# A four-layer convolution stack on one core: order of the first pair's statistics, and of work inside the last pair's layers 2 and 3

## The chip, the core and the metric

The kernel runs on one core of one Trainium2 chip. A core has four engines that compute side by side, each with its own instruction queue: PE (TensorE, matrix products; its loads of weights are listed apart as PEld), DVE (VectorE), ACT (ScalarE) and POOL (GpSimd). SP issues most of the DMAs. The metric is the time of one execution on the device in microseconds, the median of several runs. All data are float32.

## What is computed

The input is a batch of 8 images of 64 channels and 128 x 128 pixels. Four layers follow each other, each added to its input, and each fed with a group norm (32 groups, so two channels of one image share mean and variance):

```python
# layer 0: "adder" 3x3 convolution, for every output channel o
x = x + relu(b[o] - sum(abs(patch - w[o])))
# layer 1: per channel, silu and a cubic B-spline of 8 coefficients
x = x + scale_base * silu(v) + scale_sp * spline(v) + bias
# layer 2: Haar transform to four subbands, depthwise 3x3, pointwise 4C x 4C,
#          3x3 convolution 4C x 4C, gelu, inverse Haar
t = conv(conv(depthwise(haar(v)), pw_w), cv_w)
x = x + haar_inverse(gelu(t))
# layer 3: nearest of 512 codes of 64 channels for every pixel
d = (v*v).sum() + (e*e).sum() - 2 * (v @ e.T)
x = x + e[argmin(d)]
```

Each group norm needs the statistics of the whole image before the first element of its layer can be computed.

## The kernel before

Two images of 64 channels fill the 128 partitions, so the batch is four pairs, taken one after the other by `run` (L1233). An image of 128 rows is cut into NCH = 8 chunks of R = 16 rows for all but layer 0, which uses chunks of 32 rows.

**The frame.** `setup` (L120) prepares the weights of all layers inside one memory pool named setup (L187): first the constants and layer 0's weights and bias (w0, w0o, b0, up to L209), then layer 1's (cf, l1w, stored to DRAM at L261), layer 2's (cvn and pwn are loaded, 36 blocks are copied to wsrc, transposed on PE and copied back to cvt, L302 to L305; the pointwise and the 3x3 weights are multiplied to w2, L318, and w2 is stored to DRAM, L321; then gam, L335), and the code book (embT, esq_half, L345 to L359). After setup, `run` takes the statistics of pair 0: `raw_norm` (L397) loads the raw image in 8 tiles of 1 MB through three buffers (L403), takes bn_stats of each (L419) and combines them to mean and inverse deviation in mr (`group_norm_steps`, L433). It loads the first chunk of layer 0 into x0 and normalizes it there (`pad_first`, L508). Then each pair goes through layer 0 (`layer0`, L512) and layer 1 (`layer1`, L698). For all pairs but the last, layers 2 and 3 and the raw statistics of the next pair run as small steps in between the next pair's layer 0 (`layer2_beside`, `layer3_beside`), at steps written out by hand. The last pair has no layer 0 after it, so its layers 2 and 3 run alone, in `layer2` (L804) and `layer3` (L915).

**Who sets the order.** In layer 0 the instructions of PE, ACT and DVE stay in the order of the program. Elsewhere the framework plans the order for each engine when it builds the kernel: it walks through a time of its own estimate and, when an engine is free, takes the instruction that comes first in the program among those that it deems ready. A later instruction can so be put ahead of an earlier one that would still wait; the chip then carries out that order whatever really comes first. Memory of a pool that is closed is given to the pools opened after it.

**Layer 2 of the last pair.** For each chunk, `transform` (L836) makes the four subbands (8 rows of 64 columns each) in `sub`, a padded tile with a border row above and below, two of them in turn. `border` (L832, POOL copies) fills border rows from the neighbouring chunk. `depthwise` (L849) takes 9 operations for each subband, one scaling and eight multiply-adds, over 8 rows into `dw`. The first and last row of dw that the 3x3 convolution needs beyond the chunk are again copied by `border` from the neighbour's dw. `convolve` (L862) accumulates 9 taps x 4 subbands x 2 images for each half of the output channels (oab), each product of 64 x 512; taps are the outer loop, subbands the inner one:

```python
for n, (di, dj, w) in enumerate(taps):
    for k in range(4):
        for i, rows in enumerate(images):
            v = dw[rows, k, di : di + G, dj : dj + S]
            nc.tensor.matmul(ps[:, i], self.w2[rows, k, w, oab, :], v, ...)
```

In the trace each such product is two instructions. `inverse` (L882) is another 16 products and four additions into x. The loop (L893 on) makes the transform of chunk j + 1 and the depthwise of chunk j before the convolution of chunk j - 1.

**Layer 3 of the last pair.** For each chunk, x is normalized to xn (DVE), squared to sq (ACT), and 16 products with two columns sum the squares over channels (px, PE, L929), which DVE halves to xsq (L931). Then, for each of 16 rows and both images: a product with the code book into ps (PE, L938; four PSUM buffers, pool pd), t = half the code's square plus xsq (ACT, L941), nd = ps - t with its maximum (DVE, L944), the index of the maximum ix (DVE, L946), and a gather of the codes into g by POOL (L947). After each row the gathered codes of both images are transposed on PE into q (L955), and after each fourth row DVE adds q to x (L958). The chunk is stored at its end.

Of the kernel before, what the change touches and what calls it, by code (L numbers as in the profile page):

```python
# [22 lines left out]
C = 64  # L23
# [77 lines left out]
class Net:  # L101
    def __init__(self, ctx, tc, x, w0, b0, coef, sbase, ssp, bias1, dw_w, dw_b, pw_w, pw_b, cv_w, cv_b, embed, out):
        self.tc, self.nc = tc, tc.nc
        self.embed = embed
        self.n_pairs = x.shape[0] // 2
        self.x_dram = x.rearrange("(n two) c h w -> n (two c) (h w)", two=2)
        self.out_dram = out.rearrange("(n two) c h w -> n (two c) (h w)", two=2)
        self.dram = ctx.enter_context(tc.tile_pool(name="dram", bufs=1, space=bass.MemoryType.DRAM))
        self.const = ctx.enter_context(tc.tile_pool(name="const", bufs=1))
        self.small = ctx.enter_context(tc.tile_pool(name="small", bufs=2))  # L110
        self.s_of = [self.dram.tile([2, RA + 2, W + 2], F32, name=f"s{n}_dram") for n in range(2)]
        self.x_of = [self.dram.tile([P, H * W], F32, name=f"x{n}_dram") for n in range(3)]
        self.setup(w0, b0, coef, sbase, ssp, bias1, dw_w, dw_b, pw_w, pw_b, cv_w, cv_b, embed)
# [6 lines left out]
    def setup(self, w0, b0, coef, sbase, ssp, bias1, dw_w, dw_b, pw_w, pw_b, cv_w, cv_b, embed):  # L120
# [66 lines left out]
        with tc.tile_pool(name="setup", bufs=1) as sp, tc.tile_pool(name="setup_ps", bufs=2, space=PSUM) as pp:  # L187
# [13 lines left out]
            for n in range(len(PLANS)):  # L201
# [7 lines left out]
                nc.vector.tensor_tensor(self.b0[:, n], ws, braw, ALU.add)  # L209

# [593 lines left out]
    def layer2(self, mr, stats):  # L804


        nc, tc = self.nc, self.tc
# [5 lines left out]
        with ExitStack() as ctx:  # L813
# [9 lines left out]
            def padded(name, bufs, j):  # L823
                t = sp.tile([P, 4, G + 2, S + 2], F32, name=name, tag=name, bufs=bufs)
                nc.gpsimd.memset(t[:, :, :, 0 : S + 2 : S + 1], 0.0)
                if j == 0:
                    nc.gpsimd.memset(t[:, :, 0, 1 : S + 1], 0.0)
                if j == NCH - 1:
                    nc.gpsimd.memset(t[:, :, G + 1, 1 : S + 1], 0.0)
                return t  # L830

            def border(above, below):  # L832
                nc.gpsimd.tensor_copy(above[:, :, G + 1, 1 : S + 1], below[:, :, 1, 1 : S + 1])
                nc.gpsimd.tensor_copy(below[:, :, 0, 1 : S + 1], above[:, :, G, 1 : S + 1])

            def transform(j):  # L836
                t = padded("sub", 2, j)
                xv = self.x[j]
                s, d = (sp.tile([P, R, S], F32, name=n) for n in ("hs", "hd"))
                nc.vector.tensor_tensor(s, xv[:, :, 0:W:2], xv[:, :, 1:W:2], ALU.add)  # L840
                nc.vector.tensor_tensor(d, xv[:, :, 0:W:2], xv[:, :, 1:W:2], ALU.subtract)
                at = (slice(1, G + 1), slice(1, S + 1))
                nc.vector.scalar_tensor_tensor(t[:, 0, at[0], at[1]], s[:, 0:R:2], m4, s[:, 1:R:2], ALU.add, ALU.add)
                nc.vector.tensor_tensor(t[:, 1, at[0], at[1]], s[:, 0:R:2], s[:, 1:R:2], ALU.subtract)
                nc.vector.tensor_tensor(t[:, 2, at[0], at[1]], d[:, 0:R:2], d[:, 1:R:2], ALU.add)
                nc.vector.tensor_tensor(t[:, 3, at[0], at[1]], d[:, 0:R:2], d[:, 1:R:2], ALU.subtract)
                return t

            def depthwise(j, sub):  # L849
                t = padded("dw", 3, j)  # L850
                for k in range(4):
                    out = t[:, k, 1 : G + 1, 1 : S + 1]
                    for n, (di, dj, w) in enumerate(taps):
                        v = sub[:, k, di : di + G, dj : dj + S]
# [7 lines left out]
            def convolve(j, dw, oab):  # L862
# [6 lines left out]
                for n, (di, dj, w) in enumerate(taps):  # L869
                    for k in range(4):  # L870
# [3 lines left out]
                    if n == 0:  # L874
# [18 lines left out]
            sub = transform(0)  # L893
            dw = late = None
            for j in range(NCH + 1):
                done = dw
                if j < NCH:
                    if j + 1 < NCH:
                        below = transform(j + 1)
                        border(sub, below)  # L900
                    dw = depthwise(j, sub)
                    sub = below
                    if j > 0:
                        border(done, dw)
                if j > 0:
                    gs = [convolve(j - 1, done, 0)]
                    if late is not None:
                        inverse(*late)
                    gs.append(convolve(j - 1, done, 1))
                    late = (j - 1, gs)  # L910
# [4 lines left out]
    def layer3(self, mr, pair):  # L915
        nc, tc = self.nc, self.tc
        with ExitStack() as ctx:
# [4 lines left out]
            for j in range(NCH):  # L922
                xn = sp.tile([P, R, W], F32, name="xn")
                self.normalize(xn, self.x[j], mr)
                sq = sp.tile([P, R, W], F32, name="sq")
                nc.scalar.activation(sq, xn, AF.Square)
                px = pq.tile([P, 2 * R], F32, name="px", tag="px")
                for r in range(R):
                    nc.tensor.matmul(px[:, 2 * r : 2 * r + 2], sq[:, r, :], self.per_image, start=True, stop=True)  # L929
                xsq = sp.tile([P, 2 * R], F32, name="xsq")  # L930
                nc.vector.tensor_scalar(xsq, px, 0.5, None, ALU.mult)  # L931
                for r in range(R):
                    g = tp.tile([P, 2, C], F32, name="g")
                    for img in range(2):
                        rows = slice(img * C, (img + 1) * C)
                        n = 2 * r + img
                        ps = pd.tile([P, NE], F32, name="ps")
                        nc.tensor.matmul(ps, xn[rows, r, :], self.embT[rows, :], start=True, stop=True)  # L938
                        t = tp.tile([P, NE], F32, name="t")

                        nc.scalar.activation(t, self.esq_half, AF.Identity, bias=xsq[:, n : n + 1])  # L941
                        nd = tp.tile([P, NE], F32, name="nd")
                        mx = self.best[:, n % NB, :]
                        nc.vector.tensor_tensor_reduce(nd, ps, t, 1.0, -FAR, ALU.subtract, ALU.max, mx[:, 0:1])  # L944
                        ix = tp.tile([P, 8], U32, name="ix")
                        nc.vector.max_index(ix, mx, nd)  # L946
                        nc.gpsimd.indirect_dma_start(  # L947
                            out=g[:, img, :],
                            out_offset=None,
                            in_=self.embed,  # L950
                            in_offset=bass.IndirectOffsetOnAxis(ap=ix[:, 0:1], axis=0),
                        )
                    if r % 4 == 0:
                        q = pq.tile([P, 4, W], F32, name="q", tag="q")
                    nc.tensor.transpose(q[:, r % 4, :], g.rearrange("p i c -> p (i c)"), self.ident)  # L955
                    if r % 4 == 3:
                        v = self.x[j][:, r - 3 : r + 1, :]
                        nc.vector.tensor_tensor(v, v, q, ALU.add)  # L958
                cols = slice(j * R * W, (j + 1) * R * W)
                nc.sync.dma_start(out=self.out_dram[pair][:, cols], in_=self.x[j].rearrange("p r w -> p (r w)"))  # L960
# [272 lines left out]
    def run(self):  # L1233
        tc = self.tc
        mr = self.mr_tile()
        later = None
        with ExitStack() as first:
            self.x0 = first.enter_context(tc.tile_pool(name="x0", bufs=1)).tile([P, (RA + 2) * (W + 2)], F32, name="x0")
            for _ in self.raw_norm(0, mr):
                pass  # L1240
            self.load_chunk(0, 0, self.x0)
            self.pad_first(mr)
            for pair in range(self.n_pairs):
                last = pair + 1 == self.n_pairs
                stats, nxt = self.stats_tile(), self.mr_tile()
                raw, count = (iter(()), 2) if last else (self.raw_norm(pair + 1, nxt), 2 * NCH + 8)
                plans = [3] + [1] * 7 + [2] * 6 + [0] * 2 if later else [0] * NP
                counts = [TILES[n] // 2 if n else 0 for n in plans[:-2]] + [count // 2] * 2
                if later is None:
                    self.layer0(pair, mr, stats, BUFS_ALONE, lambda p: (plans[p], raw, counts[p]))  # L1250
                else:
                    with tc.tile_pool(name="between", bufs=1) as bp:
                        between = bp.tile([P, NCH * 4, 6], F32, name="between")
                        steps = chain(self.layer2_beside(later, between, sum(counts[:8])), self.layer3_beside(between, pair - 1, sum(counts[8:-2])), raw)
                        self.layer0(pair, mr, stats, BUFS_BESIDE, lambda p: (plans[p], steps, counts[p]))
                if last:
                    first.close()
                else:
# [45 lines left out]
```

## Time and profile before

| | us |
|---|---|
| median of 3 runs (19237.88 to 19248.91) | 19244.84 |
| the profiled execution | 19248.76 |
| its span, first to last instruction | 19247.0 |
| first operation of layer 0 (ACT) starts at | 133.48 |
| layer 2 of the last pair, about | 18168 to 18800 |
| layer 3 of the last pair, about | 18800 to 19247 |

Busy time in these stretches, and the mean clock granted to PE (1 is full speed):

| stretch, us | PE | DVE | ACT | POOL | clock |
|---|---|---|---|---|---|
| 0 to 133 | 58.4 | 55.4 | 22.5 | 13.4 | 0.86 |
| 133 to 4000 | 3825.0 | 3799.2 | 3677.2 | 196.2 | 1.00 |
| 18168 to 18800 | 586.3 | 273.6 | 19.1 | 28.3 | 0.97 |
| 18800 to 19247 | 392.9 | 362.7 | 185.3 | 245.8 | 0.59 |

The page gives busy time per engine, the chain of waits followed back from the last instruction, and groups of instructions with their mean duration and the idle time ahead of them. A record of an instruction is named by its line, engine and operation, with what it writes and reads. PE's matrix products are pipelined and their ends are modelled, so a PE that is busy all the time may still work slowly.

### The profile page before, as it was taken

To read this page: it belongs to the slowest core of one execution; us is meant where nothing else is said; L and a number is where in the kernel's file an instruction comes from. 1 tells how busy PE (TensorE), PEld (TensorE's weight loads), DVE (VectorE), ACT (ScalarE), POOL (GpSimd) and SP (SyncE) were. 2 spreads that over 40 slices of the span, in tenths; PEclk is the share of its full clock that TensorE was granted. 3 is DMA by queue.
4 is the path that set the end of the run, shared out by engine and by line. 5 is a ranking of instruction groups with operands and counts; after the bars stand their busy time and mean duration, and the time that the engine had idled before them with its cause. 6 is when DMAs were issued, how large, how long until landed. Compare 5 with 4: busy or idle time off the path is not lost.

```text
span 19247.0 us, 328577 instructions
## 1 busy us (share of the span) xinstructions
PE 18582.4 (97%) x145850; PEld 5795.2 (30%) x145850; DVE 17869.9 (93%) x13785; ACT 17302.3 (90%) x6401; POOL 2775.6 (14%) x1698
## 2 busy tenths in 40 slices
PE   8999999999999999999999999999999999999898
PEld 2333233233233222222223222222232322222343
DVE  8999999989999999998999999998899999999837
ACT  7999999889999999988999999998999999999603
POOL 0000000000000344200000034420000004441005
PEclk9999999999999999999999999999999999999996
DMA  1000000121111000021111100002011110000101
GB/s 52 6 11 10 6 12 8 43 63 37 36 33 37 20 20 27 26 73 35 34 41 35 33 15 24 24 28 82 28 33 38 35 33 19 23 22 16 59 1 35
DMA packets 412639, 584.02 MB, mean 30 GB/s; under 512 B 64080, under 2 KB 309456, under 8 KB 385744
## 3 DMA queue, kind: packets, MB, share of 16 engines
q1 hardware_dynamic: 355408, 497.90, 8.6%
q0 software_dynamic: 55808, 65.11, 1.9%
q8 instruction: 1142, 18.71, 0.4%
q14 instruction: 281, 2.30, 0.0%
HBM read 439.55 MB, written 123.25 MB: 29 GB/s over the span
## 4 chain that ended last, share of the span: by engine, by line
PE 54%; DVE 27%; issue 9%; ACT 8%; DMA 1%; POOL 0%; SPq 0%; DVEq 0%; ACTq 0%; POOLq 0%
PE ps L691 39%; DVE buf L624 12%; DVE buf L628 9%; ACT buf L622 7%; PE cv L1066 5%; PE pa L787 2%; PE pb L787 2%; PE ps L873 2%; DVE dw L1043 1%; DVE ix L1193 1%; DVE nd L1191 1%; PE ps L938 1%; DVE x L624 1%; PE py L1089 1%; PE pd L1179 1%
## 5 line engine op out<-in xcount | busy, mean ns | idle before, releaser
L691 PE MATMUL ps<-buf,sel 128*32 128x512 f32 x116336 | 13032.1, 598 | 358.4 <-DVE buf L628 233.4
L622 ACT ACTIVATE buf<-buf,w 128x4096 f32<-128x4096 f32 x1980 | 7212.9, 3708 | 305.9 <-PE ps L691 299.5
L622 ACT ACTIVATE buf<-x,w 128x4096 f32<-128x4096 f32 x1938 | 7044.5, 3708 | 376.5 <-PE ps L691 290.8
L691 PEld LDWEIGHTS ps<-buf,sel 128*32 128x32 f32 x116336 | 3642.9, 110 | 9338.4 <-issue 7867.1
L624 DVE TENSOR_SCALAR buf<-buf,w 128x4096 f32<-128x4096 f32 x1795 | 4162.7, 2357 | 193.7 <-PE ps L691 192.9
L624 DVE TENSOR_SCALAR buf<-x,w 128x4096 f32<-128x4096 f32 x1558 | 3640.1, 2367 | 284.3 <-PE ps L691 274.5
L628 DVE SCALAR_TENSOR_TENSOR buf<-buf,w,buf 128x2048 f32<-128x2048 f32 x1262 | 2913.5, 2349 | 23.0
L628 DVE SCALAR_TENSOR_TENSOR buf<-x,w,buf 128x2048 f32<-128x2048 f32 x1072 | 2475.3, 2349 | 19.7
L1194 POOL DMA_INDIRECT g<-in_L_conv_embed_weight,ix x768 | 1825.6, 2377 | 2849.3 <-issue 1432.4
L602 POOL DMA_DIRECT2D y<-in_x x480 | 608.3, 2072 | 9442.6 <-ACT y L589 6467.9
L1066 PE MATMUL cv<-dw,w2s 64*128 64x512 f32 x6912 | 1655.2, 607 | 3.3 <-issue 3.3
L622 ACT ACTIVATE x<-buf,w 128x4096 f32<-128x4096 f32 x396 | 1468.6, 3709 | 60.8 <-PE ps L691 60.7
L691 PE MATMUL ps<-x,sel 128*32 128x512 f32 x10832 | 1302.8, 595 | 27.1 <-DVE x L628 18.9
L1066 PEld LDWEIGHTS cv<-dw,w2s 64*128 64x128 f32 x6912 | 628.0, 186 | 1025.4 <-issue 1012.0
L624 DVE TENSOR_SCALAR x<-buf,w 128x4096 f32<-128x4096 f32 x281 | 660.2, 2349 | 24.4 <-PE ps L691 24.2
L691 PEld LDWEIGHTS ps<-x,sel 128*32 128x32 f32 x10832 | 352.6, 110 | 849.1 <-issue 742.7
L1043 DVE SCALAR_TENSOR_TENSOR dw<-sub,dws,dw 128x512 f32<-128x512 f32 (+2 forms) x768 | 574.9, 749 | 10.6
L873 PE MATMUL ps<-dw,w 64*128 64x512 f32 x2304 | 525.5, 597 | 29.4 <-DVE dw L859 20.4
L1191 DVE CUSTOM_DVE_ANT_0 nd<-pd,t 128x512 f32<-128x512 f32 x768 | 520.0, 677 | 30.5 <-ACT t L1181 30.4
L1193 DVE FIND_INDEX8 ix<-best,nd 128x8 uint32<-128x512 f32 x768 | 526.1, 685 | 0.1
L776 DVE TENSOR_TENSOR r<-r,r 128x1024 f32<-128x1024 f32 x384 | 455.0, 1219 | 76.1 <-ACT r L775 76.1
L1179 PE MATMUL pd<-embT,xn 64*128 64x512 f32 x1536 | 491.4, 650 | 30.0 <-DVE best L1191 29.6
(220 smaller groups left out, 7961.3 us busy)
## 6 DMA issues: line engine op xcount, KB each, us to landing
w2s<-w_dram SPq DMA_DIRECT2D x576, 192.0 KB
xd<-x_dram SPq DMA_DIRECT2D x256, 256.0 KB
x<-x_dram SPq DMA_DIRECT2D x56, 1024.0 KB
raw<-in_x SPq DMA_DIRECT2D x32, 1024.0 KB
x_dram<-y SPq DMA_DIRECT2D x512, 64.0 KB
out<-x SPq DMA_DIRECT2D x32, 1024.0 KB
y<-in_x POOLq DMA_DIRECT2D x480, 64.0 KB, 4.2
x_dram<-x SPq DMA_DIRECT2D x24, 1024.0 KB
```

The lines of the kernel that those rows point to most:

```text
L622: nc.scalar.activation(ab, tap(j, ts[0]), AF.Abs, bias=w[:, ts[0] : ts[0] + 1], scale=-1.0)
L624: nc.vector.tensor_scalar(ab, tap(j, ts[0]), w[:, ts[0] : ts[0] + 1], None, ALU.max)
L628: nc.vector.scalar_tensor_tensor(at, tap(j, t, h), w[:, t : t + 1], at, ALU.max, ALU.add)
L691: nc.tensor.matmul(at, sel[:, M - 1 - m : 3 * M - 1 - m], rhs, start=(n == first[p]), stop=(n + 1 == first[p + 1]))
L787: nc.tensor.matmul(to[images[i], q, :], dspl[:, k, ws[i], :], cubes[i][:, cols], start=(p == 0), stop=stop)
L873: nc.tensor.matmul(ps[:, i], self.w2[rows, k, w, oab, :], v, start=(n == 0 and k == 0), stop=(n == 8 and k == 3))
L1043: nc.vector.scalar_tensor_tensor(out, v, wt, out, ALU.mult, ALU.add)
L1066: nc.tensor.matmul(ps[:, i], weights[r, w // 3, :], v, start=(k == 0 and n == 0), stop=(k == 3 and n == 8))
L1179: nc.tensor.matmul(ps, xns[j][at, r, :], self.embT[at, :], start=True, stop=True)
L1191: nc.vector.tensor_tensor_reduce(nd, ps, t, 1.0, -FAR, ALU.subtract, ALU.max, mx[:, 0:1])
L1193: nc.vector.max_index(ix, mx, nd)
L1194: nc.gpsimd.indirect_dma_start(out=g[:, img, :], out_offset=None, in_=self.embed, in_offset=bass.IndirectOffsetOnAxis(ap=ix[:, 0:1], axis=0),)
```

## The change

It has three parts. (1) The statistics of the first pair, the load of x0 and its normalization move from `run` into `setup`, right after layer 0's bias and ahead of the weights of layers 1 to 3; x0's pool is opened before setup. (2) In layer 2 of the last pair `sub` becomes one tile that reaches four image rows (two subband rows) into the next chunk, and `depthwise` of chunk 0 covers one row more, of later chunks the same number shifted by one; a chunk's first two dw rows are copied from the chunk before. The depthwise of chunk j + 1 is issued before the convolution of chunk j, and subbands become the outer loop of the convolution. (3) In layer 3 of the last pair the sums of squares of chunk j + 1 are issued at row 6 of chunk j (`prepare`) and taken at row 12 (`take_squares`); the transposes and the addition of four rows come six rows after the last of them (`add`, LATE = 6), with 12 buffers of g instead of 4 and 8 of ix.

```diff
@@ __init__
+        self.first = ctx.enter_context(ExitStack())
+        self.x0 = self.first.enter_context(tc.tile_pool(name="x0", bufs=1)).tile([P, (RA + 2) * (W + 2)], F32, name="x0")
         self.setup(w0, b0, coef, sbase, ssp, bias1, dw_w, dw_b, pw_w, pw_b, cv_w, cv_b, embed)
@@ setup, after the bias b0
+            self.mr0 = self.mr_tile()
+            for _ in self.raw_norm(0, self.mr0):
+                pass
+            self.load_chunk(0, 0, self.x0)
+            self.pad_first(self.mr0)
@@ layer2
-            def padded(name, bufs, j):
...
-            def border(above, below):
-                nc.gpsimd.tensor_copy(above[:, :, G + 1, 1 : S + 1], below[:, :, 1, 1 : S + 1])
-                nc.gpsimd.tensor_copy(below[:, :, 0, 1 : S + 1], above[:, :, G, 1 : S + 1])
+            sub = sp.tile([P, 4, G + 3, S + 2], F32, name="sub")
+            dws_of = [sp.tile([P, 4, G + 2, S + 2], F32, name=f"dw{n}") for n in range(3)]
+            for t in [sub] + dws_of:
                 nc.gpsimd.memset(t[:, :, :, 0 : S + 2 : S + 1], 0.0)
+            for t in (sub, dws_of[0]):
+                nc.gpsimd.memset(t[:, :, 0, 1 : S + 1], 0.0)
+            inner = slice(1, S + 1)
+
+            def transform(j):
+                if j > 0:
+                    nc.vector.tensor_copy(sub[:, :, 1:3, inner], sub[:, :, G + 1 : G + 3, inner])
+                row = 3 if j else 1
+                for n, lo, hi in ((j, 4 if j else 0, R), (j + 1, 0, 4)):
+                    if n == NCH:
+                        nc.vector.memset(sub[:, :, row, inner], 0.0)
+                        continue
+                    xv = self.x[n][:, lo:hi]
+                    s, d = (sp.tile([P, R, S], F32, name=name)[:, 0 : hi - lo] for name in ("hs", "hd"))
+                    nc.vector.tensor_tensor(s, xv[:, :, 0:W:2], xv[:, :, 1:W:2], ALU.add)
+                    nc.vector.tensor_tensor(d, xv[:, :, 0:W:2], xv[:, :, 1:W:2], ALU.subtract)
...
+            def depthwise(j):
+                t = dws_of[j % 3]
+                if j > 0:
+                    nc.gpsimd.tensor_copy(t[:, :, 0:2, inner], dws_of[(j - 1) % 3][:, :, G : G + 2, inner])
                 if j == NCH - 1:
+                    nc.gpsimd.memset(t[:, :, G + 1, inner], 0.0)
+                at, n_rows = (1, G + 1) if j == 0 else (2, G - 1 if j == NCH - 1 else G)
                 for k in range(4):
-                    out = t[:, k, 1 : G + 1, 1 : S + 1]
+                    out = t[:, k, at : at + n_rows, inner]
                     for n, (di, dj, w) in enumerate(taps):
-                        v = sub[:, k, di : di + G, dj : dj + S]
+                        v = sub[:, k, at - 1 + di : at - 1 + di + n_rows, dj : dj + S]
...
-                for n, (di, dj, w) in enumerate(taps):
-                    for k in range(4):
+                for k in range(4):
+                    for n, (di, dj, w) in enumerate(taps):
...
-                    if n == 0:
+                    if k == 0:
                         for r, c, e in ends:
...
+            transform(0)
+            dw = depthwise(0)
+            late = None
+            for j in range(NCH):
                 done = dw
+                if j + 1 < NCH:
+                    transform(j + 1)
+                    dw = depthwise(j + 1)
+                gs = [convolve(j, done, 0)]
+                if late is not None:
+                    inverse(*late)
+                gs.append(convolve(j, done, 1))
+                late = (j, gs)
             inverse(*late)
@@ layer3: normalize, Square and the px products move into prepare(j), the
@@ halving into take_squares(j), the body of the row loop into nearest(j, r)
+                g = gs[j, r] = tp.tile([P, 2, C], F32, name="g", bufs=LATE + 6)
...
+                    ix = tp.tile([P, 8], U32, name="ix", bufs=8)
...
+            def add(j, r):
+                q = pq.tile([P, 4, W], F32, name="q", tag="q")
+                for n in range(4):
+                    nc.tensor.transpose(q[:, n, :], gs.pop((j, r + n)).rearrange("p i c -> p (i c)"), self.ident)
+                v = self.x[j][:, r : r + 4, :]
+                nc.vector.tensor_tensor(v, v, q, ALU.add)
+                if r + 4 == R:
+                    cols = slice(j * R * W, (j + 1) * R * W)
+                    nc.sync.dma_start(out=self.out_dram[pair][:, cols], in_=self.x[j].rearrange("p r w -> p (r w)"))
+
+            prepare(0)
+            take_squares(0)
+            for n in range(NCH * R + LATE):
+                j, r = divmod(n, R)
+                if j + 1 < NCH and r in (6, 12):
+                    (prepare if r == 6 else take_squares)(j + 1)
+                if j < NCH:
+                    nearest(j, r)
+                if n >= LATE + 3 and (n - LATE - 3) % 4 == 0:
+                    add(*divmod(n - LATE - 3, R))
@@ run: the loop over pairs is unchanged but for the lines moved to setup
-        mr = self.mr_tile()
-        later = None
-        with ExitStack() as first:
-            self.x0 = first.enter_context(tc.tile_pool(name="x0", bufs=1)).tile([P, (RA + 2) * (W + 2)], F32, name="x0")
-            for _ in self.raw_norm(0, mr):
-                pass
-            self.load_chunk(0, 0, self.x0)
-            self.pad_first(mr)
+        mr, later = self.mr0, None
```

## The prediction

> **What bounds the kernel now.** I read the page first, then the busy time by stage, then the three places that the diff touches.
>
> ```profile
> span 19247.0 us, 328577 instructions
> PE 18582.4 (97%) x145850; PEld 5795.2 (30%) x145850; DVE 17869.9 (93%) x13785; ACT 17302.3 (90%) x6401; POOL 2775.6 (14%) x1698
> PEclk9999999999999999999999999999999999999996
> ```
>
> The lines are busy time, share of the span and instructions of each engine, and the clock granted to PE in tenths, in 40 slices. Three engines are nearly full, but that is layer 0, which the diff leaves alone; only the last slice, with layer 3 in it, has a low clock. The windows by stage give what it can reach: 133 us before the first layer-0 operation, 632 us of layer 2 of the last pair (18168 to 18800), 447 us of its layer 3 (to 19247). These parts follow each other, so a microsecond saved in one is one saved in all.
>
> Start. The chain of waits over the first 140 us (start, us, what):
>
> ```profile
> 85.04 7.93 PE gp L335 x36
> ...
> 96.35 1.59 PE ep L357 x2
> 97.96 4.68 DMA raw<-in_x
> ...
> 116.95 13.80 DMA x<-in_x
> 130.85 2.56 DVE x L485
> 133.48 3.72 ACT buf L622
> ```
>
> The weights of all layers are prepared first, up to 97.9; only then do the raw image and its statistics come, and layer 0 starts at 133.48. The DMA queue's own waits say why the image is late (us in total, times, longest):
>
> ```profile
> SPq L321 <- ACT w L319: 40.3, 1, 40.3
> SPq L403 <- DMA w_dram<-w: 11.9, 1, 11.9
> ```
>
> The raw loads (L403) are queued behind the store of w2, and their buffers lie in memory that the setup pool gives back only at its end: the store has landed and ep is done at 97.9, and so are both waits.
>
> Layer 2. PE by itself, in order of time (start, us, and in brackets its idle time before and who ended it):
>
> ```profile
> 18194.35 5.38 PE L873 MATMUL ps<-dw,w 64*128 64x512 f32 x16 [14.52 <-DVE dw L859]
> 18205.61 3.79 PE L873 MATMUL ps<-dw,w 64*128 64x512 f32 x8 [5.88 <-DVE dw L859]
> ...
> 18237.02 14.81 PE L873 MATMUL ps<-dw,w 64*128 64x512 f32 x56 [8.95 <-POOL dw L833]
> ```
>
> The sums of chunk 0 start at 18194.35 and stop twice: with the tap as outer loop the first taps want all four subbands, and the taps of the last row want a border row which is copied from chunk 1. From 18252 to the last inverse PE hardly waits (541 busy of 544 us).
>
> Layer 3. Who waited for whom, 18800 to the end, and one repeated place of PE and DVE:
>
> ```profile
> DVE x L958 <- PE q L955: 34.7, 29, 4.3
> ...
> DVE nd L944 <- PE ps L938: 32.3, 7, 4.8
> ```
> ```profile
> 18871.81 6.98 PE L929 MATMUL px<-per_image,sq 128*128 128x2 f32 x32
> ...
> 18878.72 2.08 PE L938 MATMUL ps<-embT,xn 64*128 64x512 f32 x4
> ...
> 18880.94 0.69 DVE L944 CUSTOM_DVE_ANT_0 nd<-ps,t 128x512 f32<-128x512 f32 x1 [4.58 <-PE ps L938]
> ```
>
> DVE is the engine that does the work here: two nd and two ix per row come every 2.54 us. It loses 34.7 us to additions that are queued before their codes have arrived, and 32.3 us to PE, which needs 6.98 us for one chunk's sums of squares while DVE has only four ready products (pd, four buffers) to live on. The px blocks come every 54.2 us ((19142.78 - 18871.81) / 5).
>
> **The Trainium skill.** "DMA: Bandwidth & Descriptors", Bandwidth, Measured: 1 MB from HBM takes 6.15 us, 341 GB/s. Here 100 to 120 us moves 383 GB/s, a little more; I use that. "TensorE: Matmul & The Clock Gate", Part 1: the array runs at half clock until it has been busy for a window of some 3.4 us. Layer 2 agrees: a clock of 0.67 until 18205, 0.82 to 18252, 1.00 after. In layer 3 it is 0.59, although PE's row there is hardly ever empty, so I don't count on a release. "Perfetto Trace Analysis", Optimization Strategy: a gap that repeats can mean too few buffers. The 4.58 us gap, the same at each chunk, is such a one, and the change adds no pd buffer. "SBUF — State Buffer", Who interferes with whom: a DVE instruction with two SBUF inputs contends with a GpSimd read. POOL's copies of 128x256 do spread from 0.40 to 2.47 us beside L859.
>
> **The change, part by part.**
>
> Start: nothing is added; 8 raw loads, 32 bn_stats, the group norm, the load of x0 and its normalization move ahead of the other weights. The block that is exposed now is 133.48 - 97.96 = 35.5 us, and that is the most that can go. Least: nothing, if the weights are pushed back by as much. On SP the loads go past all later weight loads (cvn among them), and past the store of l1w, for which SP already stands 5.7 us. On POOL go x0's memsets (three seen, 0.16 to 0.21 us each) and the power of mr (0.58 us), between setup's own, which are done by 13.3 us; PE gets two small products (0.56 us) and the wait for the statistics in front of them, behind which tp and wp may stand. That risk is in the delay below. Once w0o is in (19.4), 8 raw (8.4 MB), x0 (2.2 MB) and the remaining weights (about 3 MB) at 0.383 MB/us take 36 us, to about 55; bn_stats of a tile takes 2.47 us, as long as its load, so DVE is nearly full until then, with wsrc (L302, 8.7 us), l1w and the like in the gaps. The first cvn was used at 38.8, and from there to ep it is 59 us, nearly all PE. I put that first use at about 51, so setup ends at 110, layer 0 starts at 111, and the part saves 22 us (0 to 35). The rest of x0's 13.8 us is hidden with it. Layer 0's other buffers still wait for the setup pool's end.
>
> Layer 2: chunk 0 now reaches one row further (128x576), so it needs no row of chunk 1. STT of that shape takes 0.818 us in the second pair's L1043 against 0.748, so it starts every 0.735 instead of 0.668. With k outermost PE can start when subbands 0 and 1 are done (the planner runs them in pairs, as now): 2 x 0.56 + 16 x 0.735 = 12.9 us after dw begins. dw begins at 18183.0 now, after parts of chunk 1's transform (hs and hd, some 2.4 us, and three sub, some 1.9) have run between the steps of the group norm; in their place come six small operations of 128 to 256 elements, some 2 us, so about 2 us earlier: PE starts at 18193.7. The 72 products of k = 0 and 1 take 15.5 us, by when k = 2 and 3 are ready. The 160 products until 18252.0 took 57.7 us; without stops they take 160 x 0.216 + 0.6 of edges = 35.1, and some 3 us of slow clock. That is 19.6 us and 0.7 of the earlier start: 20 us (14 to 23). The pad memsets come once instead of per chunk (0.2 us each on POOL, hidden by the group norm). Later chunks: a copy of sub on DVE (0.42 us in L1015) and doubled POOL copies, under 5 us, beside 72 us of PE per chunk: nothing. DVE has chunk 1 ready at about 18238, PE wants it at 18259.
>
> Layer 3: the additions move six rows on, some 15 us, while a code is late by 1 to 2 us now. Of 34.7 us, 4.3 is the last one, which stays: 30.4 go. POOL issues two gathers per row, 1.245 us each: 2.49 under DVE's 2.54, so it is not next. What is late next is PE. The px block stays: 32 instructions in 6.98 us at this clock, then 2.08 for the next pair, against four products: 4.58 us again, wherever in the chunk it stands. xsq is taken 15 us after its start instead of at the end, but DVE waited for px once only (7.9 us, the first, which stays), so that hides nothing new. The stores of a chunk on SP come six rows later; only the last one is exposed, and it still follows the last addition. PE's sum at this clock is 16 x (2.08 + 0.41) + 6.98 = 46.8 us per chunk; DVE's is 16 x 2.54 + 4 x 0.61 + 1.6 = 44.7, with the px wait 49.3. PE also stops for g, 36.1 us in all by the same waits, as long as the planner puts each transpose where it expects the code and not where the program has it; part of this comes back to DVE. I take 4 us of 30 for it: 26 us. Bounds: 0 if every q wait turns into a ps wait, 58 if PE's clock rises and the px waits go too.
>
> Sum: 22 + 20 + 26 = 68. Profiled: 19248.8, less 68 is 19180.8; it stands 3.9 above the median of the three runs (19244.8), so 19177.
>
> **Rivals.** (1) Setup is pushed back by as much as the statistics take: the DMAs and DVE speak for it, the idle DMA of 56 to 84 us against. 0 + 20 + 26: 19199. (2) In layer 3 PE takes DVE's place: 92% busy now, 18870 to 19200, at half clock speaks for it; against it, DVE waits for ps only behind px. 22 + 20 + 3: 19200. (3) The px waits go as well, because PE, less held up, is granted more clock; for it, some pairs already run in 1.1 us, against it 20 us of unbroken work at 2.0: 22 + 20 + 58: 19145. (4) Slower: transposes fall between the two products of a row, which then run singly at 2.07 us each instead of 2.08 for both; three rows from 18864 show it. A share f of such rows makes the chunk 46.8 + 33 f us. It cancels the 42 us of the other parts from 59.4 us per chunk (f = 0.38) and is over 0.2% slower beyond f = 0.53. At f = 0.7 it is 69.9: 126 us lost, 19329. (5) The planner puts the instructions where it did before: layers 3 and the start gain nothing, 19225.
>
> **Numbers.** Likeliest 0.50; (1) 0.13, (2) 0.15, (3) 0.14, (4) 0.03, (5) 0.05. The range 19145 to 19212 takes in the bounds of the three parts but not all at once. A measurement can tell 0.2%, 38.5 us: all but (4) and (5) are faster by more, with a little off the low sides of the others.
>
> **What would show it.** First ACT of L622 at 105 to 118, bn_stats before the wp products. First ps of layer 2 within 2 us of now, no PE wait in it until its end, and ps at full clock 4 us on. L958's waits under 6 us in all; ps waits of 4.6 us once per chunk, px blocks some 50 us apart. I am wrong if layer 0 starts after 125, if ps waits grow beyond 50 us, or if px blocks stay 54 us apart.

## The result and the profile after

The changed kernel takes 19213.5 us (median of 20 runs, 19205.6 to 19223.5), the kernel before 19244.7 (20 runs, 19235.9 to 19256.9): a ratio of 0.9984, 95% interval 0.9978 to 0.9990. That is 31 us less where 68 were forecast, and just outside the forecast range of 19145 to 19212. The profiled execution took 19208.65 us, 40 less than that of before. From the page:

```profile
span 19206.9 us, 328705 instructions
PE 18497.7 (96%) x145850; PEld 5765.4 (30%) x145850; DVE 17886.6 (93%) x13835; ACT 17301.5 (90%) x6401; POOL 2765.7 (14%) x1664
PEclk9999999999999999999999999999999999999996
```

By stage, with the first ACT operation of layer 0 and the two aggregates of statistics that frame layer 2 (L464 before, L474 after) as marks:

| stage | before | after | gain | forecast |
|---|---|---|---|---|
| until layer 0's first ACT operation | 133.5 | 126.75 | 6.7 | 22 |
| layers 0 and 1, unchanged | 18039.8 | 18028.7 | 11.1 | 0 |
| layer 2 of the last pair | 626.3 | 621.6 | 4.7 | 20 |
| layer 3 of the last pair | 447.4 | 429.9 | 17.5 | 26 |

The second row is scatter: in two profiles made later on one chip it was 18034.3 before and 18035.7 after, and in all 14 profiles of this document it lies between 18025.9 and 18039.8. The other three add up to 28.9, and each is short of its forecast.

**Start.** The chain of waits of the changed kernel (start, us, what):

```profile
26.29 8.32 DVE stats L429 x14
...
37.50 12.03 DMA x<-in_x
49.63 0.83 DVE x L495
...
63.81 3.65 DMA pwn<-in_L_conv_pw_w
67.82 0.49 PE tp L314
...
124.14 2.09 PE ep L367 x2
126.75 1.93 ACT buf L632
```

The statistics and x0 are done by 52, long before they are needed. But the chain of setup starts at 67.8, where it started at 39.1 before, and from there it is the same 58 us to ep. So 28.7 of the 35.5 us came back. What SP issues meanwhile (start, us, what), and its waits in the first 140 us:

```profile
16.47 20.98 SPq L413 DMA_DIRECT2D raw<-in_x  x8
...
38.18 7.70 SPq L233 DMA_DIRECT2D cf<-in_L_conv_coef  x1
...
61.90 0.59 SPq L302 DMA_DIRECT2D cvn<-in_L_conv_cv_w  x1
```
```profile
SPq L413 <- DVE stats L429: 13.3, 5, 5.3
SPq L271 <- DVE l1w L260: 5.3, 1, 5.3
```

SP is busy with the eight raw loads until 37.5, since it stands 13.3 us there for the three raw buffers and 4.3 us more for a raw tile. The first load of cf, right behind x0, then takes 7.7 us to issue where it took 0.5 before; the profile shows no wait for it, but the DMA engines are full at that time (busy share 1.0 from 30 to 46). Together that is some 29 us. The later weight loads, cvn among them, stand behind it and take as long as before: some 0.6 us for each issue, and a wait for l1w that is not new (5.3 us, 5.7 before).

**Layer 2.** PE by itself (py is what the inverse's products write, in four positions that DVE adds to x one by one):

```profile
18174.45 10.63 PE L891 MATMUL ps<-dw,w 64*128 64x512 f32 x36 [13.66 <-DVE dw L877]
...
18271.12 1.94 PE L906 MATMUL py<-g,idwt 128*64 128x512 f32 x8
18272.99 1.12 PE L891 MATMUL ps<-dw,w 64*128 64x512 f32 x2
18286.80 3.68 PE L906 MATMUL py<-g,idwt 128*64 128x512 f32 x8 [12.69 <-DVE x L908]
...
18298.89 6.70 PE L891 MATMUL ps<-dw,w 64*128 64x512 f32 x29
```

The two stops at the beginning are gone as forecast: PE comes to chunk 0's inverse 119.1 us after the first hs, where it took 141.0. There it stops for 12.69 us, and then runs slowly: from 18271.1 the inverse takes 27.8 us. In the kernel before it took 10.6:

```profile
18310.81 1.94 PE L888 MATMUL py<-g,idwt 128*64 128x512 f32 x8
...
18319.58 1.94 PE L888 MATMUL py<-g,idwt 128*64 128x512 f32 x8
18321.44 2.41 PE L873 MATMUL ps<-dw,w 64*128 64x512 f32 x9
```

DVE in the changed kernel at that time:

```profile
18253.01 0.53 DVE L875 TENSOR_SCALAR dw<-sub,dws,dwb 128x512 f32<-128x512 f32 x1
18253.58 6.26 DVE L877 SCALAR_TENSOR_TENSOR dw<-sub,dws,dw 128x512 f32<-128x512 f32 x8
...
18276.15 4.69 DVE L877 SCALAR_TENSOR_TENSOR dw<-sub,dws,dw 128x512 f32<-128x512 f32 x6
...
18286.06 0.68 DVE L908 TENSOR_TENSOR x<-x,py 128x512 f32<-128x512 f32 x1
```

These are the depthwise sums of chunk 3, 33 us with parts of the transforms of chunks 4 and 5 between, and chunk 0's first addition (L908) is queued behind them. PE starts the second position of py only when that addition has read the first. In the kernel before, the sums of chunk 3 stood ahead of that addition too, but later against PE, after a wait for the buffer that chunk 0's convolution was still reading:

```profile
18279.80 1.09 DVE L857 TENSOR_SCALAR dw<-sub,dws,dwb 128x512 f32<-128x512 f32 x2 [9.40 <-PE ps L873]
```

**Layer 3.** Who waited for whom, 18777 to the end:

```profile
DVE nd L963 <- PE ps L957: 49.5, 14, 6.3
DVE xsq L949 <- PE px L945: 7.9, 1, 7.9
DVE x L978 <- PE q L976: 4.3, 1, 4.3
```

Of the 34.7 us of waits for q only the last, 4.3 us, is left, as forecast. But the waits for ps grew from 32.3 to 49.5. PE at the place that repeats:

```profile
18861.16 0.45 PE L976 MATMUL q<-ident,g 128*128 128x128 f32 x1 [3.49 <-DMA g<-in_L_conv_embed_weight,ix]
18861.53 2.08 PE L957 MATMUL ps<-embT,xn 64*128 64x512 f32 x4
18863.54 6.99 PE L945 MATMUL px<-per_image,sq 128*128 128x2 f32 x32
18870.46 2.08 PE L957 MATMUL ps<-embT,xn 64*128 64x512 f32 x4
```

In PE's queue every transpose stands three rows behind the products, but the one just ahead of px only two, and its code is late. PE stands 3.5 to 4.2 us there, and so reaches px with less of its lead: DVE waits 0.9 to 1.5 us ahead of the block and 6.27 after it, where it was 4.6. The px blocks come every 52.0 us ((19123.66 - 18863.54) / 5), not 54.2 and not 50.

### The profile page after: what moved, and what is told of

Same layout as the page of the kernel before. It is cut to its first block, busy times and chain, and to the rows that moved or that the text cites. A ratio compares the mean times of both kernels' runs of the same rounds, so it can differ in the third digit from the quotient of the medians.

```text
span 19206.9 us, 328705 instructions
## 1 busy us (share of the span) xinstructions
PE 18497.7 (96%) x145850; PEld 5765.4 (30%) x145850; DVE 17886.6 (93%) x13835; ACT 17301.5 (90%) x6401; POOL 2765.7 (14%) x1664
## 4 chain that ended last, share of the span: by engine, by line
PE 54%; DVE 28%; issue 10%; ACT 7%; DMA 1%; SPq 0%; POOL 0%; DVEq 0%; ACTq 0%; POOLq 0%
PE ps L701 39%; DVE buf L634 12%; DVE buf L638 9%; ACT buf L632 6%; PE cv L1099 5%; PE pa L797 2%; PE pb L797 2%; PE ps L891 1%; DVE dw L1076 1%; DVE nd L1224 1%; DVE ix L1226 1%; PE pd L1212 1%; PE py L1122 1%; DVE x L634 1%; PE pa L799 1%
## 5 line engine op out<-in xcount | busy, mean ns | idle before, releaser
L1076 DVE SCALAR_TENSOR_TENSOR dw<-sub,dws,dw 128x512 f32<-128x512 f32 (+2 forms) x768 | 574.7, 748 | 10.6
L891 PE MATMUL ps<-dw,w 64*128 64x512 f32 x2304 | 521.8, 594 | 13.7 <-DVE dw L877 13.7
L1212 PE MATMUL pd<-embT,xn 64*128 64x512 f32 x1536 | 489.0, 650 | 29.0 <-DVE best L1224 28.7
```

Source lines behind the costliest of these rows:

```text
L891: nc.tensor.matmul(ps[:, i], self.w2[rows, k, w, oab, :], v, start=(n == 0 and k == 0), stop=(n == 8 and k == 3))
L1076: nc.vector.scalar_tensor_tensor(out, v, wt, out, ALU.mult, ALU.add)
L1212: nc.tensor.matmul(ps, xns[j][at, r, :], self.embT[at, :], start=True, stop=True)
```

## The experiments

All are edits of the changed kernel. They ran on three chips (A, B, C), on each beside runs of the kernel before: 19248.9 us on A, 19245.1 on B, 19246.8 on C. So medians are compared with these, and stages only with stages on the same chip.

| run | chip | median us | less than before there | first ACT | layer 2 | layer 3 |
|---|---|---|---|---|---|---|
| weights first | A | 19195.9 | 53 | 94.4 | 621.6 | 446.7 |
| two dw | A | 19215.2 | 34 | 127.9 | 604.4 | 445.3 |
| six pd | A | 19203.8 | 45 | 128.9 | 621.6 | 416.0 |
| q after | A | 19214.0 | 35 | 127.9 | 621.5 | 427.4 |
| changed, again | B | 19231.2 | 14 | 126.9 | 621.5 | 443.5 |
| py split | B | 19189.4 | 56 | 125.3 | 582.2 | 443.8 |
| px spread | B | 19204.1 | 41 | 127.2 | 621.5 | 421.5 |
| weights first, two dw, six pd | B | 19149.8 | 95 | 93.5 | 604.3 | 415.1 |
| before, again | C | 19248.6 | -2 | 134.5 | 626.3 | 448.2 |
| changed, a third time | C | 19218.8 | 28 | 126.7 | 621.5 | 430.2 |
| weights first, py split, six pd | C | 19099.3 | 148 | 95.3 | 582.2 | 389.1 |
| the same, px spread, q after | C | 19089.4 | 157 | 95.1 | 582.2 | 379.2 |

**Weights first.** The block of loads of dww, dwb, pwn, cvn and b2 goes ahead of the raw ones:

```diff
+            with nc.allow_non_contiguous_dma("weights, once"):
...
+                        nc.sync.dma_start(out=pwn[rows, ab, :], in_=pwv[k])
+                        nc.sync.dma_start(out=cvn[rows, ab, :, :], in_=cvv[k])
...
             self.mr0 = self.mr_tile()
             for _ in self.raw_norm(0, self.mr0):
                 pass
```

> The changed kernel, but SP issues the loads of dww, dwb, pwn, cvn and b2 before the eight raw loads and x0 (all parts of the change stay). Theory: the setup chain was pushed back 28.7 us only because cvn stands on SP behind the raw loads, which wait for the three raw buffers (13.3 us) and for l1w (5.3 us), and not because data or DVE lack. Then the first wsrc copy starts at 36 to 45 instead of 67.5, the chain after it keeps its 58 us, and layer 0's first ACT operation comes at 98 to 108 instead of 126.7: 19 to 28 us less than the changed kernel, some 19187 to 19194. Rival A (DVE: bn_stats and wsrc share it, so the chain stretches by the 20 us of bn_stats): first ACT at 115 to 122. Rival B (the DMA engines are the limit): the raw loads end later by what cvn takes and x0 is last, first ACT no earlier than 120.

PE's first transpose, and the end of the chain at the start:

```profile
29.35 2.97 PE L314 MATMUL tp<-ident,wsrc 128*128 128x128 f32 x7 [4.97 <-DVE wsrc L312]
```
```profile
80.47 13.55 DMA w_dram<-w
94.36 2.29 ACT buf L632
```

Layer 0 starts at 94.4, 32.4 us before the changed kernel and a little more than the theory allowed, since cvn is now in at 29. bn_stats and the weights' copies do share DVE: PE waits some 6 us for DVE's copies, and the chain is 64 us instead of 58, which costs little. Rivals A and B fall; the order on SP was the cause. What ends last now is the store of w2, which no longer has the raw loads behind it but still holds the setup pool.

**Two dw buffers.**

```diff
-            dws_of = [sp.tile([P, 4, G + 2, S + 2], F32, name=f"dw{n}") for n in range(3)]
+            dws_of = [sp.tile([P, 4, G + 2, S + 2], F32, name=f"dw{n}") for n in range(2)]
-                t = dws_of[j % 3]
+                t = dws_of[j % 2]
```

> The changed kernel with two dw buffers instead of three in the last pair's layer 2, so that the depthwise sums of chunk 3 can't be queued on DVE ahead of the additions of chunk 0's inverse. Theory: the expected 20 us of layer 2 were won at its start and 17 us given back at 18273, where PE stands 12.7 us for the addition of chunk 0 behind those depthwise sums and then runs some 5 us longer at a low clock. From the first hs to the statistics' aggregate it is 625.0 us in the changed kernel; without the stop 608 (606 to 610). Rival: chunk 0's stop is only the first place where DVE is behind, and with less room PE stops for dw elsewhere: 620 to 635. The rest of the kernel should keep its times.

PE at chunk 0's inverse:

```profile
18282.69 1.94 PE L906 MATMUL py<-g,idwt 128*64 128x512 f32 x8
18284.56 1.12 PE L891 MATMUL ps<-dw,w 64*128 64x512 f32 x2
18285.61 1.94 PE L906 MATMUL py<-g,idwt 128*64 128x512 f32 x8
```

No stop: layer 2 is 17.2 us shorter, from the first hs 607.9 us, and no other place stops. The cause and its size are shown. The median doesn't show it because layer 3 takes 445 us on this chip; more on that below.

**py split.**

```diff
-                py = pi.tile([P, 4, G, S], F32, name="py")
                 for pos in range(4):
+                    py = pi.tile([P, G, S], F32, name="py", tag="py")
```

> The changed kernel, but the last pair's inverse in layer 2 writes four tiles py of one bank each instead of one tile of four, so that PE's products of one position don't wait for DVE's addition of the one before. Theory: that dependence is how DVE's backlog stops PE at 18273; without it PE runs through chunk 0's inverse, and layer 2 (aggregate to aggregate) falls from 621.6 to 602 us: 17 us of the stop, as with two dw buffers, and 2.4 us of the three waits of 0.79 us at the end. Rival: PE stops for DVE one step later, at the next conv or inverse: 612 to 621.

```profile
18273.80 7.09 PE L906 MATMUL py<-g,idwt 128*64 128x512 f32 x32
18280.81 8.00 PE L891 MATMUL ps<-dw,w 64*128 64x512 f32 x36
```

The stop is gone, and the gain is 39.3 us, twice what was expected. In the kernel with one py tile pairs of products (L891) stand between the positions, 1.12 us a pair where two in a row of many take 0.43, and 8 of L906 take 1.94 us where 32 take 7.09. With the four positions in one row a chunk takes 69.5 us instead of 72.2; seven times 2.75, 17.1 of the stop and 2.4 at the end are 38.8. The 2.75 us per chunk are no loss that the change brought: the kernel before has the same 1.94 and 1.12 us.

**Six pd.**

```diff
-            pd = ctx.enter_context(tc.tile_pool(name="l3_pd", bufs=4, space=PSUM))
-            pq = ctx.enter_context(tc.tile_pool(name="l3_pq", bufs=2, space=PSUM))
+            pd = ctx.enter_context(tc.tile_pool(name="l3_pd", bufs=6, space=PSUM))
+            pq = ctx.enter_context(tc.tile_pool(name="l3_pq", bufs=1, space=PSUM))
```

> The changed kernel with six ps buffers in layer 3 instead of four (q and px get one bank each instead of two). Theory: DVE's 6.27 us wait per chunk is the px block (6.98 us) less the lead that the ready products give; six products are 7.6 us of DVE work, so the wait at px falls to 0 to 2 us and a chunk takes 46.5 to 48 us instead of 52.0, by PE's own sum of 46.8 at this clock; layer 3 390 to 402 instead of 430. Rival A (PE is slow through and through, at half clock, and the lead can't be rebuilt): PE's waits for g and single products leave 50 to 52. Rival B (with one q bank the transposes wait for the additions): DVE waits for q come back, 52 to 56.

```profile
DVE nd L963 <- PE ps L957: 19.3, 9, 4.0
```

Waits for ps fall from 49 to 19.3 us and layer 3 from some 446 to 416 on this chip; a chunk takes 49.4 us. That is more than the 46.5 to 48 of the theory and just under rival A's 50; part of it may lie with the stops described at the end: on chip C, where there are none, it is 46.2 us per chunk and 9.8 us of such waits, with py split and the weights first. There rival A falls; B falls here already, since DVE waits for q in an addition only once, for the last one (3.8 us). (With one q bank the transposes also come four at a time, so the edit is not of the lead alone.)

**q after.**

```diff
+                with tc.issue_after(newest[0]):
                     for n in range(4):
                         nc.tensor.transpose(q[:, n, :], gs.pop((j, r + n)).rearrange("p i c -> p (i c)"), self.ident)
```

newest[0] is the product issued last, so the transposes stand behind the products of six rows later.

> The changed kernel with the four transposes of an addition queued on PE behind the product of six rows later, in place of one at a time as soon as the code is expected. Theory: PE's stop of 3.5 to 4.2 us for a code just ahead of each px block takes part of the lead; with it gone, the wait at px falls from 6.27 to 4.6 to 5.8 us (four transposes, 1.65 us, now stand in a row) and the extra 0.9 us before it goes: a chunk takes 49.5 to 51 us instead of 52.0, layer 3 414 to 424 instead of 430; PE's waits for g fall from 88.9 to under 10. Rival (the px block alone sets the wait): chunk stays at 52.

```profile
DVE nd L963 <- PE ps L957: 32.5, 8, 4.8
```

DVE's waits for ps fall to 32.5 us; the wait at px is 4.8 us at most, those ahead of it are gone, and PE waits 7.0 us for g in all. A chunk takes 51.0 us, at the end of what was expected, and layer 3 427.4, a little over it; the two other runs with the unchanged layer 3 on this chip have 53.7 us per chunk. The rival falls: 17 us of the waits for ps came from where the transposes stood. The edit moves all of them; that the one just ahead of px did the harm is read from the trace, where DVE's waits stand only around px.

**px spread.** prepare(j + 1) at row 0 without its products, and then one row of them behind each row's own. The edit of "q after" is in it too:

```diff
+                if j + 1 < NCH and r > 0:
+                    for row in ((0, 1) if r == 1 else (r,)):
+                        with tc.issue_after(newest[0]):
+                            squares(j + 1, row)
+                    if r == R - 1:
+                        take_squares(j + 1)
```

> The changed kernel with layer 3's sums of squares spread out: xn and sq of the next chunk at row 0, then the px product of one row behind the products of each row, and the transposes queued behind the product of six rows later. Nothing is left out. Theory: DVE's 6.27 us wait stems from the px products standing in one block of 6.98 us; spread over 16 rows they cost PE 0.44 us per row, 46.8 us per chunk in all at this clock, against 44.7 of DVE: a chunk of 46.8 to 49 us instead of 52.0, layer 3 390 to 405. Rival (PE pays for each change between the kinds of products, or the granted clock falls): 50 to 54 us per chunk, 415 to 440.

Layer 3 takes 421.5 us against 443.5 of the changed kernel on chip B, so 22 less, but not 390 to 405: the waits for a block become many short ones, with four ps buffers as before. That is in the rival's range, and the granted clock did fall, to 0.60 from 0.63. "q after" alone was worth some 18 us on chip A (445.3 and 446.7 to 427.4), so the spread by itself seems to add little here; no run has it alone.

**The changed kernel again, and the kernel before.**

> The changed kernel once more as it is. In the first execution profiled its layer 3 took 429.9 us from the aggregate of the statistics, while two runs with the same instructions there (weights loaded first; two dw buffers) took 446.7 and 445.3. Theory A (the time is a fixed property of each program): 428 to 432 again, and 621.6 for layer 2. Theory B (it varies from execution to execution with the clock that PE is granted, about 0.61 in the slow ones and 0.66 in the fast one): anything from 428 to 448. The starts and layer 2 should repeat within 1 us in both.

> The changed kernel as it is, a third time, on the same chip as the kernel before. Theory: start and layer 2 repeat within 1 us, and layer 3 lies anywhere from 428 to 448 us. If it is near 430 again, the run is some 31 us faster than the kernel before; if near 444, some 14.

> The kernel before as it is, profiled once more. If its layer 3 (447.4 us in the first profile) varies from run to run as that of the changed kernel does (429.9 and 443.5), it lies between 440 and 460; if the forecast's reading of its waits holds, DVE again waits 30 to 35 us for q and some 32 us for ps. Layer 2 626.3 and the first ACT operation of layer 0 at 133.5 should repeat within 1 us.

Start and layer 2 repeat within 1 us. Layer 3 doesn't: 429.9 and 430.2 us, but 443.5 on chip B, whose 12 runs (19226.6 to 19232.8) lie above all of the first 20. So the gain of the whole change is 31, 14 and 28 us; on B its ratio is 0.9992 (0.9984 to 1.0001), so small that the interval reaches 1, though all 12 runs there lie below all 30 of the kernel before (19239.4 to 19251.8). Theory A falls, and B in its plain form as well: the times on B differ among themselves by 6 us, and all of them from the first 20. Each of the three chips was used at one time only, so chip and time of the run can't be told apart. The kernel before has 447.4 and 448.2, with the same waits for q (34.7) and ps (32.3).

**Combinations.**

> The three edits that shortened a stage, together: weights' loads ahead of the raw ones, two dw buffers in layer 2, six ps buffers in layer 3. Theory (the stages follow each other, so their gains add): 32.8 us less at the start, 17.2 in layer 2, 14 in layer 3 against the first profiled execution of the changed kernel: 64 us, 19145 to 19160. Rival (an earlier or shorter stage is paid for in layer 3, as the runs with the first two edits seem to show, by 15 us each): layer 3 above 425 us, 19165 to 19185.

> Weights' loads first, py in four tiles, six ps buffers in layer 3. Theory (gains add): 32.8 us at the start, 39.3 in layer 2, 14 to 28 in layer 3 (415 us): against the combination with two dw buffers 22 us less, so 19125 to 19131. Rival (the shorter layer 2 is paid for in layer 3): 19140 or more.

> The same with the sums of squares spread over the rows and the transposes queued six rows behind as well, so that six ready products and no px block stand in layer 3. Theory: with no block and a deeper lead a chunk comes to PE's own sum, 46.8 us at this clock, or to DVE's 44.7: layer 3 385 to 405 instead of 415, 19100 to 19118. Rival (PE bound at half clock, with changes between kinds of products that cost it more, as 421.5 with the spread alone hints): 410 to 425, no better than the version without the spread.

The gains of start and layer 2 add to within 1 us in all three, and the rivals fall. The first combination came as expected. The other two were faster than expected, by 26 and 11 us beyond the low ends (19099.3 for 19125 to 19131, 19089.4 for 19100 to 19118), because layer 3 took 389.1 and 379.2 us on chip C where 415 and 385 to 405 had been put. The last version is 157 us faster than the kernel before (ratio 0.9917, 0.9900 to 0.9933) and is the best. Its layer 3:

```profile
DVE xsq L951 <- PE px L947: 7.9, 1, 7.9
DVE x L981 <- PE q L979: 3.7, 1, 3.7
DVE nd L965 <- ACT t L962: 1.1, 2, 0.9
```

No wait for ps is left, at a clock of 0.65; DVE is busy 358 of 379 us. So PE's rate doesn't set layer 3 once the px block is spread and the lead is six products.

## Why the prediction was wrong

**Start: the placement of cvn failed.** The step is "I put that first use at about 51": it was 67.5. The prediction listed that on SP the loads go past cvn and past l1w's store, and then added up bytes and DVE work, as if the weights' loads ran under the raw ones. They come after them: SP issues in order, and a load that waits for one of three raw buffers holds every load behind it. The moved bytes were sized well enough: 10.6 MB at the prediction's 0.383 MB/us are 27.6 us, an estimate, and they held SP for some 29. What it put at nothing is that the weights' loads are a chain of their own, of issues, the wait for l1w and the landing of cvn: 22.5 us before from the first load of cf to the first use of cvn (16.3 to 38.8), 29.3 now (38.2 to 67.5). Rival (1), pushed back by as much, was nearly right in size (28.7 of 35.5). Of its reasons the DMAs count in part, as they were full while the raw tiles came; but with the same bytes in another order layer 0 started at 94.4. The bounds, 0 to 35, held, and one of the signs of being wrong came true: layer 0 starts after 125. (The 6.15 us and 341 GB/s that the prediction cites for 1 MB don't fit each other, 1 MB in 6.15 us being some 170 GB/s; it used the trace's 383, so nothing rests on them.)

**Layer 2: the start was right, "later chunks ... nothing" failed.** Begin of the sums, readiness of subbands 2 and 3 and the end of both stops were as forecast, and worth 22 us: PE starts 22.5 us after the first hs instead of 24.5, and reaches the inverse 21.9 us earlier. But the prediction took later chunks as a matter of PE's work alone and not of DVE's order. In the kernel before DVE stood 9.4 us for PE, and was still done with chunk 3's sums 8 us before PE came to the inverse. Now PE comes 22 us earlier after the first hs; DVE, which no longer waits for the buffer, starts these sums 9 us earlier but needs 33 us with the transforms between where it needed 23. So PE meets them: 17.1 us, shown by two runs. "No PE wait in it until its end" was the line to watch, and it failed at 18286.8. The Trainium skill, "TensorE: Matmul & The Clock Gate", Part 1, says that an idle window brings half clock until one window of some 3.4 us is busy again. The trace agrees on the half clock, but not on how long it lasts: PE was granted 0.50 for 9.1 us after the stop (18286.8 to 18295.9), though busy all the time; why so long is not shown. So this stop cost more than its length: 4.4 us on top of 12.7. (One reading of the prediction was off, without harm: the long POOL copies, 2.30 and 2.47 us, ran beside hs and hd, L840 and L841, and not beside L859.)

**Layer 3: the removed wait was right, the size of what comes back was not.** 30.4 us of waits for q went, to the tenth. "I take 4 us of 30 for it" was the mis-sized term: 17.2 us came back as waits for ps. (The gain is 17.5 and not 13.2 mostly because DVE's own busy time fell from 363.0 to 359.5 us, which the prediction had not counted on.) The prediction had seen that the planner puts each transpose where it expects the code, but said "4.58 us again, wherever in the chunk it stands", as if PE always reached px with four products ready. It was 6.27 and 0.9 to 1.5, in six chunks, with one transpose a row early just ahead of px each time; moving all transposes behind the products took 17.0 us of the ps waits away. That is rival (2) in part. The signs of being wrong were just missed here: ps waits stayed under 50 us by 0.5, and px blocks at 52.0 lie between the forecast 50 and the 54 of before.

The parts fall short by 15.3, 15.3 and 8.5 us, 39 in all, and 36.5 us is what the median misses. None of the five rivals is the outcome by itself. That the parts follow each other, and that gains in them add, held.

## What to carry to other kernels

Moving loads forward on an in-order queue moves everything behind them back by the time that the queue needs for them, waits for buffers included; what stands behind doesn't run under them. So put what starts a long chain first, and what has to wait for buffers last. When a stage is made to start earlier, follow it to the next place where it meets another engine's queue, and ask what became free to run ahead there. One tile that PE writes and DVE reads position by position can tie the two engines to each other at every position; splitting it into four took 39.3 us off layer 2, more than the 28.9 of the whole change. That this is a matter of how the tile is tracked, or of the memory itself, was not told apart.

## What was not expected of the hardware

On chips A and B DVE stops in layer 3 ahead of index lookups (L965), 2 to 12 times in each of the eight profiles there, for 0.3 to 1.9 us and often about 0.65 or 1.3, mostly with nothing but its own result before to wait for; one of chip B's run of the changed kernel:

```profile
18825.88 0.09 DVE L965 MATCH_VALUE_LOAD ix<-best,nd 128x8 f32 x1 [1.92 <-issue]
```

ACT and PE stand as well, and all three go on within 0.02 us of each other. In the first two profiles and the four of chip C there is none, but for one wait of 0.64 us in the kernel before on C that the profile puts down to a gather. These stops sum to 6.2 us in that run; with 5.9 us of waits ahead of nd that the changed kernel doesn't have on C either, they are most of the 13.6 us by which its layer 3 is longer. The granted clock is 0.63 against 0.66. What makes the stops, and why by chip, stays open; the kernel before was not profiled on A or B, and its times there (19248.9 and 19245.1) don't rise.
